# Computing the B path one step further ahead of its scan in a fused convolution-attention kernel

## The chip, the cores and the metric

The kernel runs on one core of a Trainium2 chip. The metric is the device time of one execution in microseconds, median over several executions. The kernel before took 1475.62 us (median of 3 executions, 1474.55 to 1480.86; a fourth, 1480.84, puts the median at 1478.23 in the result below).

Engines: PE is TensorE (matmuls), PEld its weight loads, DVE is VectorE, ACT is ScalarE, POOL is GpSimd, SP is SyncE, which issues 971 of the 993 transfers in the trace before.

## The reference, cut to what matters

```python
x = x + conv(_gn(x), ...)                  # GroupNorm, 32 groups, then layer 0
t = tokens(x)
t = t + attn(_ln_t(t), ...)                # linear attention, no softmax
t = t + ffn(_ln_t(t), ...)                 # FFN with quantised products

def conv(x, ...):                          # per position: LayerNorm, then one projection
    proj = layernorm(x) @ W_in + b_in      # -> value u, gate g, delta d, and A, B, C (96*16 each)
    def step(h, (A, B, C, d, u, g)):       # over 4096 positions
        h = d * (A * h) + d * (B * u)
        y = g * sum_S(C * h)
    return ys @ W_out + b_out
```

The input is 4 batches x 4096 positions x 96 channels. Each batch is worked in 8 chunks of 512 positions, and each chunk in 12 tiles, because the 96 x 16 = 1536 states of a position fill twelve sets of 128 partitions. That makes 32 chunks and 384 tiles; one step of the main loop scans one tile.

## The kernel before

For each tile PE projects A, B and C (three matmuls each) into PSUM, one bank for each letter. ACT copies B from its bank to a `bu` tile in SBUF, POOL multiplies that by `du` (d times u, replicated by DMA), DVE multiplies A by d, scans, and multiplies C by the result.

```python
    def b_copy(self):                                      # ACT
        self.bu = work.tile([P, TC], F32, tag="bu", name=f"bu_{self.nm}", bufs=4)
        nc.scalar.activation(self.bu, self.b_ps, AF.Identity, bias=self.bias(0))
    def b_mul(self):                                       # POOL
        nc.gpsimd.tensor_tensor(
            self.bu, self.bu, rep["du4", self.b, self.i, self.cg], ALU.mult
        )
    def scan(self):                                        # DVE
        ...
        nc.vector.tensor_tensor_scan(
            self.h, self.a_ps, self.bu,
            0.0 if self.i == 0 else state[self.sh, self.cg], ALU.mult, ALU.add,
        )
...
        while s < K or any(q >= s for q in steps):
            ...
            if 0 <= s + 1 < K:
                tiles[s + 1].a_proj()
            if 0 <= s < K:
                tiles[s].c_proj()
            if 0 < s <= K:
                last.keep()
            if 0 <= s + 1 < K:
                tiles[s + 1].b_mul()
            if 0 <= s < K:
                last = tiles[s]
                last.scan()
            if 0 <= s + 1 < K:
                tiles[s + 1].a_mul()
            if 0 <= s < K:
                last.c_mul()
            call(s)                  # the other work due at this step: norms, gate, FFN, ...
            if 0 <= s + 2 < K:
                tiles[s + 2].b_proj()
                tiles[s + 2].b_copy()
            s += 1
```

Two pieces of the "other work" matter below. The first is LayerNorm. `rstd` is computed on POOL, `nmr` (minus mean times rstd) on DVE, and ACT normalises with both. There are three LayerNorms per chunk: c (on `z`, ahead of the projections), a (ahead of attention) and f (ahead of the FFN). The second is GroupNorm's square root, which POOL does as a power of -0.5 once per batch.

```python
    def rsqrt(dst, var, eps):
        nc.gpsimd.tensor_scalar(dst, var, eps, None, ALU.add)
        nc.gpsimd.tensor_tensor(dst, dst, mhalf[:, : dst.shape[1]], ALU.pow)
...
        def apply(self, dst, src):                         # LayerNorm
            nmr = small.tile([P, J], F32, tag="nmr", name=f"nmr_{self.nm}")
            nc.vector.scalar_tensor_tensor(
                nmr, self.mv[:, :, 0], -1.0, self.r, ALU.mult, ALU.mult
            )
            for j in range(J):
                nc.scalar.activation(
                    dst[:, j, 0:C], src[:, j, :], AF.Identity,
                    bias=nmr[:, j : j + 1], scale=self.r[:, j : j + 1],
                )
...
        def root():                                        # GroupNorm of the next batch
            gnr[b] = small.tile([P, G], F32, tag="gnr", name=f"gnr_{b}", bufs=2)
            rsqrt(gnr[b], v["w"], 1e-5)
```

Of the kernel before, what the change touches and what calls it, by code (L numbers as in the profile page):

```python
# [8 lines left out]
F32 = mybir.dt.float32  # L9
# [7 lines left out]
P = 128  # L17
# [5 lines left out]
TC = P * J  # L23
# [21 lines left out]
def conv_attn_hybrid_kernel(  # L45
# [212 lines left out]
    work = ctx.enter_context(tc.tile_pool(name="work", bufs=2))  # L258
# [269 lines left out]
    class Tile:  # L528
# [18 lines left out]
            self.b_ps = self.proj("B", w_b)  # L547

        def b_copy(self):
            self.bu = work.tile([P, TC], F32, tag="bu", name=f"bu_{self.nm}", bufs=4)  # L550
            nc.scalar.activation(self.bu, self.b_ps, AF.Identity, bias=self.bias(0))  # L551

        def b_mul(self):
# [38 lines left out]
    tiles = {}  # L592
# [193 lines left out]
    K = N * NT  # L786
# [16 lines left out]
    def call(step):  # L803

        todo = steps.get(step, [])
        n = 0
        while n < len(todo):
            fn, args = todo[n]
            fn(*args)
            n += 1  # L810

    with tc.manual_schedule():
        s = FRONT
        while s < K or any(q >= s for q in steps):
            for k in (s, s + 1, s + 2):
                if 0 <= k < K and k not in tiles:
                    tiles[k] = Tile(k)
            if 0 <= s + 1 < K:
                tiles[s + 1].a_proj()
            if 0 <= s < K:  # L820
                tiles[s].c_proj()
            if 0 < s <= K:
                last.keep()
            if 0 <= s + 1 < K:
                tiles[s + 1].b_mul()
            if 0 <= s < K:
                last = tiles[s]
                last.scan()
            if 0 <= s + 1 < K:
                tiles[s + 1].a_mul()  # L830
            if 0 <= s < K:
                last.c_mul()
            call(s)
            if 0 <= s + 2 < K:
                tiles[s + 2].b_proj()
                tiles[s + 2].b_copy()
            s += 1


# [30 lines left out]
```

## Time and profile before

| | before |
|---|---|
| median, us | 1475.62 |
| profiled span, us | 1471.2 |
| busy share PE / DVE / POOL / ACT | 92% / 82% / 54% / 47% |
| first scan starts at, us | 119.4 |
| scan's waits for POOL's bu, us | 70.2 |
| PE weight loads' waits for ACT's bu copy, us | 32.2 |

The busy share says which engine has least idle time, but not whether a given wait costs anything: a wait counts only if what follows it is late at the end. So the useful unit here is the length of a chunk, taken as the distance between the starts of every twelfth scan. I number these stretches from 0 by scan start, so that stretch 20 starts at 909.60 us in the kernel before. (The prediction's windows are cut at other points; its timeline near 901 us lies at the end of stretch 19.) Three pairs (5+6, 13+14, 21+22) hold GroupNorm's root and what follows it. The other stretches from 10 on, eighteen of them, I call late, those from 0 to 4 and 7 to 9 early. The prediction shows the lines themselves.

### The profile page before, as it was taken

The page shows a single profiled execution, that of the slowest core. Times are in us where ns is not written, and L with a number is a line of the kernel's source. Part 1 is how long each engine was busy: PE and PEld are TensorE (multiplying, and loading weights), DVE is VectorE, ACT ScalarE, POOL GpSimd, SP SyncE. Part 2 cuts the span into 40 slices and gives each one's busy share as a digit, 9 for nine tenths or more (in the row PEclk, how much of TensorE's full clock was granted, in tenths as well). Part 3 has the DMA queues.
Part 4 walks back from the last instruction along what each step waited for, and adds up shares of the span by engine and source line. Part 5 has one row for each costly group of instructions (what it writes and reads, how often), then busy time and mean ns, then how long its engine had stood idle before and what let it go on. Part 6 is the DMA issues. An engine that isn't in the chain of part 4 may idle for free.

```text
span 1471.2 us, 20878 instructions
## 1 busy us (share of the span) xinstructions
PE 1350.2 (92%) x6513; PEld 910.4 (62%) x6513; DVE 1205.1 (82%) x2295; ACT 697.5 (47%) x1573; POOL 795.0 (54%) x772
## 2 busy tenths in 40 slices
PE   5747999998999999999999999999999999999875
PEld 4615666665666666666666666666666666666552
DVE  1017999997999999988998999988999999999743
ACT  2023344342333565544555555554555555555555
POOL 4234555555554556656655555666555655555424
PEclk9559999999999999999999999999999999999955
DMA  7102222221222222211222222221222222222001
GB/s 185 27 17 61 57 61 64 63 58 38 53 54 56 64 64 59 69 46 42 58 58 51 62 69 63 60 58 39 52 54 58 56 49 54 53 58 49 11 7 43
DMA packets 82209, 80.98 MB, mean 55 GB/s; under 512 B 49899, under 2 KB 50383, under 8 KB 82098
## 3 DMA queue, kind: packets, MB, share of 16 engines
q1 hardware_dynamic: 80080, 77.22, 22.1%
q10 hardware_dynamic: 2018, 2.43, 0.7%
q8 instruction: 51, 0.84, 0.2%
q14 instruction: 60, 0.49, 0.1%
HBM read 8.72 MB, written 6.29 MB: 10 GB/s over the span
## 4 chain that ended last, share of the span: by engine, by line
PE 57%; DVE 12%; ACT 11%; issue 6%; SPq 5%; POOL 4%; DMA 3%; ACTq 0%; POOLq 0%; DVEq 0%
PE Bps L155 13%; PE Cps L155 12%; PE Aps L155 11%; PE y_ps L601 5%; SPq L487 4%; DVE h L570 4%; PE dug_ps L155 3%; DVE ch L588 3%; POOL bu L554 3%; ACT z L305 3%; PE a_ps L705 2%; ACT xn L305 2%; ACT bu L551 2%; PE o_ps L624 2%; DMA d<-d 1%
## 5 line engine op out<-in xcount | busy, mean ns | idle before, releaser
L554 POOL TENSOR_TENSOR bu<-bu,du 128x512 f32<-128x512 f32 x384 | 493.6, 1286 | 536.9 <-ACT bu L551 382.2
L570 DVE TENSOR_TENSOR_SCAN h<-Aps,state,bu 128x512 f32<-128x512 f32 x336 | 428.2, 1274 | 58.3 <-POOL bu L554 57.5
L551 ACT ACTIVATE bu<-Bps,b_bac 128x512 f32<-128x512 f32 x384 | 261.8, 682 | 430.8 <-PE Bps L155 407.0
L563 DVE SCALAR_TENSOR_TENSOR Aps<-Aps,b_bac,d 128x512 f32<-128x512 f32 x384 | 283.9, 739 | 42.8 <-PE Aps L155 42.1
L155 PE MATMUL Bps<-xs,w 128*128 128x512 f32 x768 | 272.1, 435 | 15.0 <-ACT bu L551 15.0
L588 DVE SCALAR_TENSOR_TENSOR ch<-Cps,b_bac,h 128x512 f32<-128x512 f32 x384 | 285.6, 744 | 0.1
L155 PE MATMUL Aps<-xs,w 128*128 128x512 f32 x768 | 243.7, 398 | 13.1 <-DVE h L570 13.0
L155 PE MATMUL Cps<-xs,w 128*128 128x512 f32 x768 | 248.3, 404 | 4.0 <-DVE ch L588 4.0
L155 PEld LDWEIGHTS Bps<-xs,w 128*128 128x128 f32 x768 | 128.0, 191 | 79.0 <-ACT bu L551 32.2
L155 PEld LDWEIGHTS Aps<-xs,w 128*128 128x128 f32 x768 | 144.7, 189 | 49.6 <-DVE h L570 15.7
L155 PEld LDWEIGHTS Cps<-xs,w 128*128 128x128 f32 x768 | 139.7, 189 | 53.2 <-DVE ch L588 23.7
L155 PE MATMUL Cps<-xl,w 128*128 128x512 f32 x384 | 152.5, 397 | 0.0
L155 PE MATMUL Bps<-xl,w 128*128 128x512 f32 x384 | 152.4, 397 | 0.0
L155 PE MATMUL Aps<-xl,w 128*128 128x512 f32 x384 | 152.4, 397 | 0.0
L601 PE MATMUL y_ps<-ch,fold 128*32 128x512 f32 x768 | 136.4, 605 | 0.0
L305 ACT ACTIVATE xa<-x,nmr_a,rstd_a 128x96 f32<-128x96 f32 x128 | 49.4, 457 | 112.5 <-DVE nmr_a L301 112.5
L305 ACT ACTIVATE z<-z,nmr_c,rstd_c 128x96 f32<-128x96 f32 x128 | 49.4, 457 | 80.4 <-DVE nmr_c L301 80.4
L155 PEld LDWEIGHTS Aps<-xl,w 128*128 128x128 f32 x384 | 72.4, 188 | 18.0
L155 PEld LDWEIGHTS Cps<-xl,w 128*128 128x128 f32 x384 | 72.5, 189 | 17.7
L155 PEld LDWEIGHTS Bps<-xl,w 128*128 128x128 f32 x384 | 72.7, 189 | 17.2
L743 ACT ACTIVATE hq<-hr 128x512 fp8e5<-128x512 f16 x96 | 60.6, 631 | 17.9 <-PE y_ps L749 9.4
L155 PE MATMUL dug_ps<-xs,w_dug 128*96 128x512 f32 x192 | 64.0, 415 | 5.3 <-DMA xs<-lo 4.9
(158 smaller groups left out, 1704.3 us busy)
## 6 DMA issues: line engine op xcount, KB each, us to landing
d<-d SPq DMA_DIRECT2D x384, 64.0 KB, 2.0
du<-du SPq DMA_DIRECT2D x384, 64.0 KB, 2.0
xl<-lo SPq DMA_DIRECT2D x64, 128.0 KB, 2.3
x<-in_x_dram SPq DMA_DIRECT2D x32, 192.0 KB, 2.8
out_dram<-o SPq DMA_DIRECT2D x32, 192.0 KB, 2.1
w<-w SPq DMA_DIRECT2D x18, 128.0 KB, 2.3
xs<-lo SPq DMA_DIRECT2D x32, 64.0 KB, 2.0
raw<-in_L_conv_W_in_dram ACTq DMA_DIRECT2D x3, 576.0 KB, 5.2
```

The source lines that it names most:

```text
L155: nc.tensor.matmul(ps, lhsT=wt[:, n], rhs=mv, start=(n == 0), stop=(n == 2))
L305: nc.scalar.activation(dst[:, j, 0:C], src[:, j, :], AF.Identity, bias=nmr[:, j : j + 1], scale=self.r[:, j : j + 1],)
L487: nc.sync.dma_start(t[q * 32 : (q + 1) * 32, :], src[cg * 32 : (cg + 1) * 32, :])
L551: nc.scalar.activation(self.bu, self.b_ps, AF.Identity, bias=self.bias(0))
L554: nc.gpsimd.tensor_tensor(self.bu, self.bu, rep["du4", self.b, self.i, self.cg], ALU.mult)
L563: nc.vector.scalar_tensor_tensor(self.a_ps, self.a_ps, self.bias(1), rep["d4", self.b, self.i, self.cg], ALU.add, ALU.mult,)
L570: nc.vector.tensor_tensor_scan(self.h, self.a_ps, self.bu, 0.0 if self.i == 0 else state[self.sh, self.cg], ALU.mult, ALU.add,)
L588: nc.vector.scalar_tensor_tensor(self.ch, self.c_ps, self.bias(2), self.h, ALU.add, ALU.mult)
L601: nc.tensor.matmul(y_ps[g][cg * 32 : (cg + 1) * 32, :], lhsT=fold, rhs=tiles.pop(g * NT + NCG * sh + cg).ch, start=(sh == 0), stop=(sh == ...
L624: nc.tensor.matmul(ps[:, j, :], lhsT=yg[:, j * P : (j + 1) * P], rhs=w_o, start=True, stop=True)
L705: nc.tensor.matmul(ps[:, j, :], lhsT=xa[:, j, :], rhs=rmat[b], start=True, stop=True)
L743: nc.scalar.activation(v["hq"][:, m, :], v["hr", m], AF.Copy, saturate=False)
```

## The change

The intent is to give the scan a whole step of slack towards POOL. Projection, copy and multiplication of B each move one tile ahead, in the same places of the loop, and the ring of `bu` tiles grows by one to hold the tile that now lives one step longer.

```diff
         def b_copy(self):
-            self.bu = work.tile([P, TC], F32, tag="bu", name=f"bu_{self.nm}", bufs=4)
+            self.bu = work.tile([P, TC], F32, tag="bu", name=f"bu_{self.nm}", bufs=5)
 ...
-            for k in (s, s + 1, s + 2):
+            for k in (s, s + 1, s + 2, s + 3):
 ...
-            if 0 <= s + 1 < K:
-                tiles[s + 1].b_mul()
+            if 0 <= s + 2 < K:
+                tiles[s + 2].b_mul()
 ...
-            if 0 <= s + 2 < K:
-                tiles[s + 2].b_proj()
-                tiles[s + 2].b_copy()
+            if 0 <= s + 3 < K:
+                tiles[s + 3].b_proj()
+                tiles[s + 3].b_copy()
```

## The prediction

> **What bounds the kernel now.** I read the first part of the page, then two windows of one chunk each (a chunk is 512 positions, twelve tiles, one tile a step; 32 chunks), then the costliest groups, the waits, and last the timeline of one chunk. First the engines over the span, and the windows of chunk 20 (late, with the FFN of the previous batch beside it) and chunk 3 (early, without); columns are length, then busy us of PE, PEld, DVE, ACT, POOL:
>
> ```profile
> PE 1350.2 (92%) x6513; PEld 910.4 (62%) x6513; DVE 1205.1 (82%) x2295; ACT 697.5 (47%) x1573; POOL 795.0 (54%) x772
> 891.80:932.00 40.20, 39.74 (x201) 26.20 (x200) 36.61 (x69) 22.71 (x53) 24.27 (x25) 1.00 0.26 63
> 212.95:250.74 37.79, 37.17 (x174) 24.11 (x174) 34.78 (x60) 15.23 (x38) 21.31 (x20) 1.00 0.26 62
> ```
>
> In a chunk PE is marked busy 99% (39.74 of 40.20) and DVE 91%. DVE therefore has 3.6 us of idle time per chunk and PE seems to have 0.5. POOL, which does the multiplication that the change moves, is busy 60%. The waits, each with its total in us, its count and its longest:
>
> ```profile
> POOL bu L554 <- ACT bu L551: 382.2, 184, 5.5
> DVE h L570 <- POOL bu L554: 70.2, 64, 8.2
> PEld Bps L155 <- ACT bu L551: 32.2, 65, 3.5
> PEld Cps L155 <- DVE ch L588: 23.7, 66, 0.9
> POOL bu L554 <- DMA du<-du: 14.8, 7, 7.9
> ```
>
> POOL waiting for ACT costs nothing by itself, since POOL has time. The scan (h) waits 70.2 us for POOL, and that is the wait the change aims at. PE's own waits are smaller. The timeline of chunk 20 shows how they hang together:
>
> ```profile
> 900.84 1.28 DVE L570 TENSOR_TENSOR_SCAN h<-Aps,state,bu 128x512 f32<-128x512 f32 x1 [0.98 <-POOL bu L554]
> 901.69 7.55 SPq L487 DMA_DIRECT2D du<-du  x12
> 903.35 0.15 DVE L301 SCALAR_TENSOR_TENSOR nmr_c<-mv_c,rstd_c 128x4 f32<-128x4 f32 x1
> 903.53 1.54 ACT L305 ACTIVATE z<-z,nmr_c,rstd_c 128x96 f32<-128x96 f32 x4 [2.27 <-DVE nmr_c L301]
> 904.99 0.67 ACT L551 ACTIVATE bu<-Bps,b_bac 128x512 f32<-128x512 f32 x1
> ...
> 905.70 0.30 PEld L155 LDWEIGHTS Bps<-xs,w 128*128 128x128 f32 x2 [0.50 <-ACT bu L551]
> 905.73 1.29 POOL L554 TENSOR_TENSOR bu<-bu,du 128x512 f32<-128x512 f32 x1 [2.25 <-ACT bu L551]
> 907.06 1.28 DVE L570 TENSOR_TENSOR_SCAN h<-Aps,state,bu 128x512 f32<-128x512 f32 x1 [0.95 <-POOL bu L554]
> 908.26 0.30 PEld L155 LDWEIGHTS Bps<-xs,w 128*128 128x128 f32 x2 [0.26 <-ACT bu L551]
> 908.28 1.30 POOL L554 TENSOR_TENSOR bu<-bu,du 128x512 f32<-128x512 f32 x1 [0.41 <-ACT bu L551]
> ```
>
> A late scan (900.84) makes nmr_c late; ACT, in order, waits for it and normalises z (1.54) before it copies the next B (0.67); PE waits for that copy, because B has one PSUM bank; POOL multiplies (1.29) only then, and the scan at 907.06 is late again. So in the last four steps of a chunk the B chain (ACT, POOL, scan) sets DVE's pace and takes a little from PE; elsewhere PE is limiting, and DVE waits for it. Early chunks have one such scan, and there PE pays through C's single bank:
>
> ```profile
> 226.75 1.28 DVE L570 TENSOR_TENSOR_SCAN h<-Aps,state,bu 128x512 f32<-128x512 f32 x1 [0.88 <-POOL bu L554]
> 229.39 0.30 PEld L155 LDWEIGHTS Cps<-xs,w 128*128 128x128 f32 x2 [0.65 <-DVE ch L588]
> ```
>
> [...] PEld is only 62% busy, and a matmul marked busy 0.39 us is followed by the next after 0.23 us (900.07 to 900.30), so the mark hides stalls such as the 0.50 above. I therefore count PE's stalls from the starts of its matmuls. [...] the 0.95 us before the scan does repeat, but the binding buffer for PE is B's PSUM bank, which the change leaves at one. [...] here the du copies take 2.0 from issue to landing (median, 1.9 to 3.7), so the transfer matters if the multiplication comes earlier.
>
> **The change, part by part.** It adds and removes no instruction: 384 projections, copies and multiplications stay at about 0.70, 0.69 and 1.29 us. It costs one more 2 KB-per-partition tile.
> (1) At step s, POOL multiplies tile s+2 instead of s+1, ACT copies s+3 instead of s+2, PE projects s+3. In each engine's queue these stand where they stood; only the tile number moves by one. So the scan gets one step (at least 2.5 us: scan 1.20, A 0.64, C 0.66 from start to start) of slack. The largest routine wait is 0.98 us, so nearly all of the 70.2 us should go; one of 8.2 us lies in the start and may stay.
> (2) What of it reaches the end? DVE has idle time anyway, so what counts is PE's stalls that follow from late scans. Taking for each pair of consecutive matmul groups the 10th percentile of their distance as unstalled, a late chunk loses in its last steps 0.47 us (at 905.70) and 0.24 us (at 908.26), that is 0.71. Without the 0.98 before the scan at 900.84, nmr_c comes about 0.8 earlier (its A and C are there at 901.2 and 901.9, so not the whole 0.98), the copy ends near 904.9 instead of 905.66, and PE, free near 905.2, does not wait. Then the second stall goes too, ACT's cycle (2.55 from copy to copy) being close to PE's (2.43). I find the pair in 17 late chunks, others at a batch's edges have none or part: 17 x 0.71 + 0.6 = 12.7 us.
> (3) Early chunks: C's wait for c_mul costs 0.49 us (the 0.65 of PEld, less what overlaps), in chunks 1 to 8: 8 x 0.49 = 3.9 us. B's stall there (about 0.6) comes from nmr_c with no late scan before it, and stays.
> (4) Left as they are: PE's wait for a copy after xn (0.45 of PEld at 899.49 in late chunks, nmr_f being on time), for xa (0.6 a chunk), half-clock stretches, the drain after the last scan.
> (5) The start: the first tile's du still lands at 117 us, so perhaps 1 us is gained there, which I take against the costs below.
> Sum: 12.7 + 3.9 = 16.6, some 17 us.
>
> **What may be paid.** The first multiplication of a chunk needs du, and now one step earlier. In chunk 20 the first four of the twelve du copies, issued from 901.69 at 0.63 each, land at 904.95 by the trace's landings; the multiplication started at 908.28, and takes in future the place of the one at 905.73: 0.8 us to spare. Other late chunks have from -0.7 to +0.8; early ones -0.3 to -1.3. So POOL will wait there for DMA in many chunks, 0.3 to 1.3 us, and the second and third du tiles follow 3 us apart. The scan has a whole step in hand, so this should be hidden; what POOL does behind it (centring for GroupNorm, four chunks a batch) comes later and may hold ACT some tenths: 1 to 3 us in all.
>
> **Rivals.** (A) DVE, or the chain through it, is the real bound: then all of the waits count, 70.2 - 8.2 = 62 us, and the time is near 1414. For it: the chain that ended last passes POOL's bu for 2.8% and the scan for 3.9% of the span. Against: the same chain is 57% PE, and after such stretches DVE waits 42 us for A from PE. A half-way case, with stalls after xn and in the early B also gone (about 0.45 x 20 + 0.6 x 8 = 14 us more), gives 1445.
> (B) The du transfer takes the place of the removed wait, POOL stays late over three tiles, and scans wait as before: gain 0 to 5, near 1472. For it: the landings above. Against: a step of slack remains, and POOL has 40% idle.
> (C) PE is so full that only the half of my stalls is recovered, others (xa, A) growing in their place: about 1467.
>
> **Range and chances.** 1475.6 - 17 = 1458.6; with 1 us of net start gain less costs I stay at 1459. B and C set the upper end at 1471, the half-way A the lower at 1443. Faster by over 2% needs less than 1446.1, that is more than 29 us, almost all of PE's stalls on B and C: 0.13. Slower by 2% would need a new stall of almost 1 us in every chunk, for which nothing speaks: 0.02. Within 2%: 0.85.
>
> **What would show it.** In the changed profile: the scan's wait for POOL below 15 us (step 1). PEld's wait for ACT's bu falling from 32 to about 17 us and for C's c_mul from 23.7 to below 12 (steps 2, 3). POOL's wait for du rising from 14.8 to 20 to 40 us (costs). DVE's waits for A from PE rising from 42 by tens of us, since the idle time moves from before the scan to before A: this would say that PE is the bound, and against A. The late chunk between equal points goes from 40.2 to 39.5 us. I am wrong if the scan still waits for POOL, if the time falls by over 29 us though PE's stalls as I counted them were only 17, or if ACT's copy gets later and PE's wait for it grows.

## The result, and the profile after

| | before | after |
|---|---|---|
| median, us (range, runs) | 1478.23 (1474.55 to 1480.86, 4) | 1462.09 (1459.15 to 1466.46, 4) |
| ratio (95%) | 1 | 0.9895 (0.9857 to 0.9933) |

A ratio is, to within 0.0004, the mean time of one kernel's fast runs over the mean of the other's fast runs of the same rounds, so it is not quite the ratio of the medians. The outputs are correct. The time fell by about 1%, inside the range and 3 us from the predicted value. The total came out close, but the terms of the sum did not.

**A caution first: two ways to start.** Executions of either kernel fall into two groups. Most have a mean granted clock below 0.96; of these, eight were profiled, and seven start their first scan at 118 to 121 us, one (e5_ring_only, described below) at 124.4. Some have 0.966 or more; the four profiled ones start it at 127 to 128, and in most series such runs take 5 to 7 us longer in all (kernel before in its last series: 1481.1 late, 1474.6 early; in e7c_all only 2.5). What sets their mean clocks apart lies before the first scan: each of the eight early records has a stretch of 68 or 75 us at half clock there, and none of the four late ones has. I call the two groups early and late starters; the early one is itself spread over some 6 us (1472.8 to 1479.3 for the kernel before). The profiled execution of the kernel after is one of the late starters (first scan at 127.2), that of the kernel before is not (119.4). I therefore compare from the first scan to the end, 1351.8 us before (1471.2 - 119.4) and 1337.5 after (1464.7 - 127.2): **14.3 us less**. Where times are compared below, I also give the mean of the early-start runs.

Engines and waits of the kernel after (each wait with total us, count, longest):

```profile
PE 1354.2 (92%) x6513; PEld 916.4 (63%) x6513; DVE 1217.9 (83%) x2295; ACT 697.1 (48%) x1573; POOL 794.7 (54%) x772
```

```profile
POOL bu L554 <- DMA du<-du: 87.8, 40, 7.9
DVE Aps L563 <- PE Aps L155: 71.7, 104, 5.2
PEld Bps L155 <- ACT bu L551: 32.5, 66, 4.2
PEld Cps L155 <- DVE ch L588: 16.2, 43, 0.9
DVE h L570 <- POOL bu L554: 13.7, 6, 3.4
```

The wait that the change aims at fell from 70.2 to 13.7 us, and DVE's idle time moved to A, which it gets from PE (42.1 to 71.7). But PE's wait for the B copy is what it was, 32.2 and now 32.5. So PE's largest repeated stall was not touched, although the prediction took most of its gain from there.

Where the 14.3 us came from, by stretches:

| stretches | before, us | after, us | difference |
|---|---|---|---|
| 0 to 4 and 7 to 9 (early) | 299.4 | 295.2 | -4.3 |
| 10 to 12, 15 to 20, 23 to 31 (late) | 710.9 (no. 12 40.15, no. 28 39.19) | 710.3 (no. 12 40.11, no. 28 39.15) | -0.6 |
| 5+6 | 82.27 | 79.88 | -2.4 |
| 13+14 | 87.08 | 83.22 | -3.9 |
| 21+22 | 86.00 | 83.23 | -2.8 |
| after the last scan | 86.16 | 85.81 | -0.35 |

Nine of the fourteen come from three places that the prediction had left out, and almost nothing from the eighteen late chunks. Two windows each show it; columns are length, then busy us of PE, PEld, DVE, ACT, POOL, then the granted clock, DMA share and GB/s. Before, stretches 13+14 and 20:

```profile
621.50:708.58 87.08, 81.65 (x396) 54.84 (x394) 74.72 (x143) 44.88 (x105) 51.56 (x47) 0.96 0.21 51
909.60:949.78 40.18, 39.67 (x202) 26.20 (x200) 36.59 (x69) 22.71 (x54) 24.27 (x24) 1.00 0.26 63
```

After, the same:

```profile
622.60:705.82 83.22, 79.13 (x395) 52.47 (x394) 75.34 (x144) 44.78 (x104) 51.08 (x48) 1.00 0.22 53
906.59:946.68 40.09, 39.61 (x201) 26.29 (x200) 37.25 (x70) 22.70 (x54) 24.39 (x25) 1.00 0.27 64
```

The late chunk has the same length and the same PE time, with DVE 0.66 us *busier* (36.59 to 37.25), though it does the same instructions. The other pair is 3.86 us shorter, with the clock at 1.00 in place of 0.96.

**Late chunks.** The end of a late chunk after the change (the place of the prediction's timeline at 901 us):

```profile
899.99 1.28 POOL L554 TENSOR_TENSOR bu<-bu,du 128x512 f32<-128x512 f32 x1
900.35 0.94 DVE L301 SCALAR_TENSOR_TENSOR nmr_c<-mv_c,rstd_c 128x4 f32<-128x4 f32 x1
901.32 1.55 ACT L305 ACTIVATE z<-z,nmr_c,rstd_c 128x96 f32<-128x96 f32 x4 [2.28 <-DVE nmr_c L301]
902.78 0.66 ACT L551 ACTIVATE bu<-Bps,b_bac 128x512 f32<-128x512 f32 x1
903.49 0.30 PEld L155 LDWEIGHTS Bps<-xs,w 128*128 128x128 f32 x2 [0.50 <-ACT bu L551]
```

The scan is in time, yet ACT still waits 2.28 us for nmr_c (2.27 before), and PE still waits 0.50 for the copy. What is new is nmr_c itself: an operation on 4 elements per partition takes 0.94 us, where it took 0.15. It ends at 901.29, when POOL's multiplication ends (901.27). All 32 of them, min/median/max in ns, first in the kernel before:

```profile
L301 DVE SCALAR_TENSOR_TENSOR nmr_c<-mv_c,rstd_c x32: 150/158/842, 96.3 to 1304.6; 128x4 f32<-128x4 f32 x32
```

and in the kernel after:

```profile
L301 DVE SCALAR_TENSOR_TENSOR nmr_c<-mv_c,rstd_c x32: 150/930/952, 104.1 to 1298.4; 128x4 f32<-128x4 f32 x32
```

In every late chunk of both kernels that has an nmr_c, it ends 16 to 26 ns after a POOL multiplication ends. Before the change, the late scan pushed DVE's work back so far that it reached nmr_c only at that moment, so the record showed a short instruction. After it, DVE comes some 0.8 us earlier (0.930 less 0.158) and stands there.

nmr_c reads two tensors of SBUF (mean and rstd); A's multiplication, the scan and C's multiplication read one each besides PSUM. In the kernel after, the medians of these three differ by at most 11 ns beside POOL: A's is 732 ns over the 62 that lie more than 95% inside a POOL multiplication and 739 over the 165 that meet none; the scan's is 1275 (9) and 1272 (82), C's 751 (38) and 740 (130). nmr_c's are 940 (19) and 153 (7). nmr_f, of the same form, takes 1.11 and 1.13 us the two times that it starts early in a multiplication, and ends 16 and 24 ns after it. So the wait may belong to the form with two SBUF inputs, but so far that is only an argument, and why such a form would wait the traces don't show.

**GroupNorm's root.** At one step of each of the first three batches POOL computes the root for the next batch. Before:

```profile
662.81 5.46 POOL L279 TENSOR_TENSOR gnr<-gnr,mhalf 128x32 f32<-128x32 f32 x1
...
669.53 1.28 DVE L570 TENSOR_TENSOR_SCAN h<-Aps,state,bu 128x512 f32<-128x512 f32 x1 [4.57 <-POOL bu L554]
670.87 1.18 PE L155 MATMUL Aps<-xs,w 128*128 128x512 f32 x2 [2.60 <-DVE h L570]
```

After:

```profile
663.74 5.46 POOL L279 TENSOR_TENSOR gnr<-gnr,mhalf 128x32 f32<-128x32 f32 x1
...
670.48 1.28 DVE L570 TENSOR_TENSOR_SCAN h<-Aps,state,bu 128x512 f32<-128x512 f32 x1 [3.02 <-POOL bu L554]
671.82 0.73 PE L155 MATMUL Aps<-xs,w 128*128 128x512 f32 x2 [0.53 <-DVE h L570]
```

A power on 32 columns takes 5.46 us, and the next multiplication stands behind it. The scan waited 4.57 us, and PE, whose A bank is freed by the scan, 2.60. With the lead these are 3.02 and 0.53. Before, the pair of matmuls after the gap takes 1.18 us instead of 0.73, since the clock is at half there (0.50 granted from 671.0 to 674.4 us). Such stretches last 3.413 us in the traces; the kernel before has five in mid-run (near 333, 353.5, 650.5, 671.0 and 998.6 us), the kernel after one (near 337.5). In the window of 13+14 the clock of 0.96 comes from two such stretches.

The traces show what goes before them. In the three with the old order (before, and e5_ring_only and e1c_before_nmrc, described below) PE stands 2.57 to 2.64 us at each of the three roots, and half clock follows all nine times. In the three with the new order (the change twice, e6_lead_ring4) that gap is 1.8 us at the first root and under 1.5 at the others, and no half clock follows. The remaining stretches follow another gap, of 2.32 or 2.33 us and a little earlier, in which PE waits for a GroupNorm sum from DVE (`gsq`). That gap is in all six traces; half clock follows it seven times in nine with the old order and three in nine with the new.

An estimate of what one stretch costs: 0.9 us, from pair 21+22, which is 86.00 us with one stretch (before) and 86.87 with two (e5); or 1.5, from e2c_after_nmrc and e7c_all, which have none in 13+14 and one in 21+22 (82.49 and 83.96, 80.32 and 81.85), where the change with none in either has 83.22 and 83.23. Four stretches fewer are then 3.5 to 6 of the 9.0 us. The rest I put down to the shorter waits themselves; no run separates the two.

### The profile page after: what moved, and what is told of

Read it like the earlier page. It is cut to its first block, busy times and chain, and to the rows that moved or that the text cites. A ratio compares the mean times of both kernels' runs of the same rounds, so it can differ in the third digit from the quotient of the medians.

```text
span 1464.7 us, 20864 instructions
## 1 busy us (share of the span) xinstructions
PE 1354.2 (92%) x6513; PEld 916.4 (63%) x6513; DVE 1217.9 (83%) x2295; ACT 697.1 (48%) x1573; POOL 794.7 (54%) x772
## 5 line engine op out<-in xcount | busy, mean ns | idle before, releaser
L554 POOL TENSOR_TENSOR bu<-bu,du 128x512 f32<-128x512 f32 x384 | 493.4, 1287 | 520.4 <-ACT state L580 312.2
L563 DVE SCALAR_TENSOR_TENSOR Aps<-Aps,b_bac,d 128x512 f32<-128x512 f32 x384 | 285.2, 743 | 72.4 <-PE Aps L155 71.7
L155 PE MATMUL Cps<-xs,w 128*128 128x512 f32 x768 | 245.2, 400 | 3.3 <-DVE ch L588 3.3
L155 PEld LDWEIGHTS Bps<-xs,w 128*128 128x128 f32 x768 | 127.4, 191 | 79.1 <-ACT bu L551 32.5
L155 PEld LDWEIGHTS Cps<-xs,w 128*128 128x128 f32 x768 | 140.7, 188 | 47.7 <-DVE ch L588 16.2
```

Of the source, the lines that this page charges most:

```text
L155: nc.tensor.matmul(ps, lhsT=wt[:, n], rhs=mv, start=(n == 0), stop=(n == 2))
L554: nc.gpsimd.tensor_tensor(self.bu, self.bu, rep["du4", self.b, self.i, self.cg], ALU.mult)
L563: nc.vector.scalar_tensor_tensor(self.a_ps, self.a_ps, self.bias(1), rep["d4", self.b, self.i, self.cg], ALU.add, ALU.mult,)
```

## The experiments

**Theory 1**: the late chunks gained nothing because nmr_c, as an operation with two SBUF inputs, has to wait for POOL's multiplication; where the scan's wait was, there is now this one. **Rival 1**: PE's two stalls belong to ACT's order and B's single bank as such, and nothing done to nmr_c helps; or any earlier nmr_c would have helped the kernel before too, so that it has nothing to do with the change. **Theory 2**: about 9 us come from the root on POOL. **Rival 2**: they come from the fifth ring tile, or from which executions were profiled. Runs of one series were made on the same chip with the same runs of the kernel before.

### The change again

a0_after_again is the changed kernel, unaltered, in the first series.

> The changed kernel once more, so that the others of this call have it on the same chip. Both theories: ratio to before 0.987 to 0.992 (1.0 to 1.3% less). In its trace: scan waiting for POOL about 14 us, PE loads of B waiting for ACT's copy about 32 us (unchanged), nmr_c with a median of about 0.93 us where before had 0.16. The profiled run of the change began its first scan 7.8 us later than the one of before; if that was chance, the first scan is here near 119 us and the span near 1457 us.

Measured: 1466.64 us (1461.82 to 1467.31), ratio 0.9927 (0.9905 to 0.9948), against 1475.55. Four of the six runs were late starters. The profiled run was again one of them (first scan at 126.8), and with them the ratio just misses the 0.987 to 0.992 that I expected. The other two have a mean of 1461.9 us and those of the kernel before 1475.7 (10 of 11): 13.8 us, near the trace's 14.3. So a few late starts move a median by 5 us. Over both series the five early-start runs of the changed kernel have a mean of **1461.4**, which I compare with from here on.

### Theory 1: nmr without the second SBUF input

The first form changes all three LayerNorms of the changed kernel. The rstd becomes a per-partition scalar of four one-column operations (label e2_after_nmr):

```diff
-            nc.vector.scalar_tensor_tensor(
-                nmr, self.mv[:, :, 0], -1.0, self.r, ALU.mult, ALU.mult
-            )
+            for j in range(J):
+                nc.vector.tensor_scalar(
+                    nmr[:, j : j + 1], self.mv[:, j, 0:1], self.r[:, j : j + 1], -1.0,
+                    ALU.mult, ALU.mult,
+                )
```

> The changed kernel, with the LayerNorm's small product nmr (mean times rstd, two SBUF tensors of 128x4) made by four tensor_scalar operations that read one SBUF tensor each and take rstd as a per-partition scalar. Theory (nmr_c is held up by POOL's multiplication[...]): the four end within 0.4 us of c_mul, the normalisation of z begins about 0.8 us earlier against the scan, the two PE stalls at the end of a late chunk (0.5 and 0.25 us of load wait) go, a late chunk falls from 40.1 to 39.4 us, and the time is 10 to 13 us below the changed kernel (ratio to before about 0.981). Rival (nmr_c waits for POOL's result or for ACT[...]): the operations start 0.8 us later instead of lasting longer, late chunks stay at 40.1 us, and the time is the changed kernel's, within 0.3%.

Measured: 1456.99 us, ratio 0.9882; early-start mean 1456.3, so 5.1 us below the change. Late chunk no. 12 fell from 40.11 to 39.77. The direction is that of theory 1, the size half of it: the end of a chunk gained 0.70, but 0.37 were lost elsewhere. The four operations take 0.55 us where nmr_f, which met at most the last tenths of a POOL multiplication in these chunks, had taken 0.13 to 0.26; so the f LayerNorm, on PE's path in another step, became later. A sharper edit was needed: only LayerNorm c, `ln.apply(v["t"], v["t"], True)`, the other two as they were. This was put on the changed kernel (e2c_after_nmrc) and on the kernel before (e1c_before_nmrc):

```diff
-        def apply(self, dst, src):
+        def apply(self, dst, src, one_input=False):
...
+            if one_input:
+                ...                          # the four tensor_scalar as above
+            else:
+                ...                          # the one scalar_tensor_tensor
...
-        at(s + 7, lambda: ln.apply(v["t"], v["t"]))
+        at(s + 7, lambda: ln.apply(v["t"], v["t"], True))
```

> The changed kernel with the product nmr made by four one-input operations for the z LayerNorm alone, the two others as they were. In the run with all three, PE's stalls at the end of a late chunk went (0.70 us a chunk), but 0.37 us came back before the transposes of xn, because nmr_f took longer. Theory [...]: without that a late chunk falls from 40.13 to about 39.4 us and the time, at an early start, from 1461.9 to about 1449 (12 to 14 us less, ratio to before about 0.982). Rival (the gain of that run came from the xn and xa norms starting after the first of four pieces): no more gained than there, ratio 0.988 or more.

> The same four operations in the kernel before. Theory: there c_mul, held back by the scan's wait for POOL, ends just when POOL's multiplication does, [...] the change of nmr gains nothing or loses up to 5 us (ratio 0.999 to 1.004), late chunks stay at 40.1 to 40.4. So neither the change nor this alone helps late chunks; both together do. Rival (the nmr form is a gain of its own, apart from the change): 10 us or more gained here too, ratio under 0.994.

Measured: on the change 1449.17 us, ratio 0.982 (0.9801 to 0.9839), all four runs early starters with a mean of 1448.9: **12.5 us** below the change. On the kernel before: 1474.9, ratio 1.0004 (0.9984 to 1.0024), nothing. The end of a late chunk in e2c_after_nmrc:

```profile
885.22 1.28 POOL L561 TENSOR_TENSOR bu<-bu,du 128x512 f32<-128x512 f32 x1
885.58 0.57 DVE L303 TENSOR_SCALAR nmr_c<-mv_c,rstd_c 128x1 f32<-128x1 f32 x4
885.82 1.54 ACT L312 ACTIVATE z<-z,nmr_c,rstd_c 128x96 f32<-128x96 f32 x4 [1.54 <-DVE nmr_c L303]
...
888.11 0.42 PEld L155 LDWEIGHTS Bps<-xs,w 128*128 128x128 f32 x2
```

POOL multiplies from 885.22 to 886.50; nmr_c starts beside it at 885.58 with 0.2 us a piece, and z starts after the first piece. ACT's wait is 1.54 instead of 2.28, and PE's load at 888.11 has no wait behind it where 0.50 stood. The late chunk is 39.38 us (no. 12) instead of 40.11 and 38.42 (no. 28) instead of 39.15, 0.73 in both. Over all eighteen late stretches the traces give 11.8 us (710.3 to 698.5), against 12.5 in the time. PE's loads wait 20.8 us for the B copy in all, where the change alone had left 32.5. So these are the stalls of 0.71 that the prediction had counted, and nmr_c's wait for POOL's multiplication was what had kept them. And e1c shows that nmr_c's form alone is worth nothing while the scan is late: no. 12 is 40.20 there. The late scan and this wait each cover the other; only removing both pays. Rival 1 falls in both forms.

### A second step of lead

If POOL were not multiplying at all when nmr_c comes, the original two-input form should be short as well. One more step of lead changes what POOL does there (e8_lead2; the ring stays at five, and in its trace a copy never starts less than 3.3 us after the end of the scan that frees its tile):

```diff
-            if 0 <= s + 2 < K:
-                tiles[s + 2].b_mul()
+            if 0 <= s + 3 < K:
+                tiles[s + 3].b_mul()
 ...
-            if 0 <= s + 3 < K:
-                tiles[s + 3].b_proj()
-                tiles[s + 3].b_copy()
+            if 0 <= s + 4 < K:
+                tiles[s + 4].b_proj()
+                tiles[s + 4].b_copy()
```

> The changed kernel with B one further step ahead (multiplied three steps before its scan, copied four), still with a ring of five. Theory (a first step of lead takes every routine wait away; what is left for a second is the rest of the waits at the three batch edges, about 3 us each in the changed kernel): the scan's waits for POOL after the start go, 2 to 6 us are gained on the changed kernel (ratio 0.986 to 0.9895), late chunks stay at 40.1 us. Rival (lead as such is short, also in late chunks): a late chunk falls below 39.8 us and 8 us or more are gained.

Measured: 1460.8 us, ratio 0.9886, mean 1460.9 (all six early). This series was run on another chip, where the kernel before has 1474.6; so the gain is 13.7 us, against 14.3 for the change (1475.7 to 1461.4), and none of the 2 to 6 us that I expected on top. (The ratio looks better because six of its eleven runs of the kernel before were late starters.) But the equality hides two opposite moves, and my expectation for the late chunks was wrong too. The end of a late chunk:

```profile
897.38 0.15 DVE L301 SCALAR_TENSOR_TENSOR nmr_c<-mv_c,rstd_c 128x4 f32<-128x4 f32 x1
...
900.47 1.30 POOL L554 TENSOR_TENSOR bu<-bu,du 128x512 f32<-128x512 f32 x1 [3.41 <-DMA du<-du]
```

POOL stands from 897.06 to 900.47 and waits for the chunk's first du, the two-input nmr_c takes 0.15 us in that time, and the late chunk without GroupNorm work is 38.44 (no. 28), as with e2c's edit (38.42): a third view of the same cause, without touching nmr_c. It also answers a rival to e2c, that the gain came only from z starting after the first of four pieces: here nmr_c is one piece. Chunks with GroupNorm's centring behind that wait got longer (40.68 to 41.94 for no. 10 to 12), since POOL's centring is late then and ACT, in order, waits for it before its square:

```profile
ACT sq L390 <- POOL xc L385: 42.1, 12, 4.6
```

POOL's waits for du are 178.9 us in total here, against 87.8 with one step. So a lead has a price in du, which is hidden at one step and shows at two.

### Theory 2: the root cut in four

On the kernel before (e3_before_split) and on the change (e4_after_split), the power is cut into four of 8 columns, one in each of four steps, so that a multiplication can go in between:

```diff
-            rsqrt(gnr[b], v["w"], 1e-5)
+            nc.gpsimd.tensor_scalar(gnr[b], v["w"], 1e-5, None, ALU.add)
+
+        def power(n):
+            c = slice(n * 8, (n + 1) * 8)
+            nc.gpsimd.tensor_tensor(gnr[b][:, c], gnr[b][:, c], mhalf[:, c], ALU.pow)
...
         at(e + 3, root)
+        for n in range(4):
+            at(e + 3 + n, power, n)
```

> The kernel before, with the one power of GroupNorm at a batch's edge (128x32 on POOL, 5.46 us) cut into four of 8 columns in four successive steps. Theory (at three batch edges POOL is shut for 5.46 us, the scan waits 4.6 us and PE 2.6 us, often with half clock after it; this is where most of the change's gain comes from): the scan's waits of over 2 us at the edges go, and 8 to 11 us are gained against before (ratio 0.993 to 0.9945). Rival (the gain comes from the routine waits in each chunk, and the edges only look large): under 3 us gained, ratio over 0.998.

> The changed kernel with the same cut of the power. Theory: the change has already taken two thirds of the edges' cost, so only 1 to 4 us are gained against the changed kernel (ratio to before 0.986 to 0.9885), and against the cut kernel of before the change is then worth 4 to 8 us instead of 15. Rival (routine waits carry the gain): the change is worth its full 15 us on top of the cut.

Measured: before plus cut 1465.21 us, ratio 0.9931 (0.9911 to 0.9952), early-start mean 1464.7: 11.0 below the kernel before. Change plus cut 1453.28, ratio 0.986, mean 1453.8: 7.6 below the change, more than I expected. The place in e3_before_split:

```profile
659.63 1.67 POOL L435 TENSOR_TENSOR gnr<-gnr,mhalf 128x8 f32<-128x8 f32 x1
661.27 1.29 POOL L560 TENSOR_TENSOR bu<-bu,du 128x512 f32<-128x512 f32 x1
662.60 1.28 DVE L576 TENSOR_TENSOR_SCAN h<-Aps,state,bu 128x512 f32<-128x512 f32 x1 [0.81 <-POOL bu L560]
```

The scan waits 0.81 us where it waited 4.57, and stretch 13 is 44.15 us instead of 48.03 (42.31 with the change). By the traces the cut takes 10.2 us from the three pairs (82.27, 87.08 and 86.00 become 78.86, 83.17 and 83.12) and leaves early and late stretches as they were. So the cut alone recovers about what the change recovers there, 9.0, by another way, and the mechanism of theory 2 holds.

My accounting for the two together was too simple, however. I expected them to overlap almost wholly at the roots, so that the change on top of the cut would be worth 4 to 8 us. It is worth 10.9 by the means (1464.7 to 1453.8) and 10.1 by the traces: 4.4 in the early stretches, 3.4 in the pair 5+6 (78.86 to 75.44), 1.1 in the other two pairs, 0.7 late and 0.6 in the drain. The excess sits at the first root: the trace of e3 has a half-clock stretch there (0.91 over 320 to 340 us), and that of e4 has none. By the estimate above that is worth 0.9 to 1.5 of the 3.4, and two early chunks at some 0.5 each (4.4 over eight) are another 1.1; the rest, about 1 us, I can't explain from one trace of each.

### The ring and the order, each alone

e5_ring_only is the kernel before with `bufs=5`; e6_lead_ring4 is the changed kernel with `bufs=4`.

> The kernel before with a ring of five bu tiles and the old order. Theory: in the trace of before, ACT's copy never comes within 6.6 us of the end of the scan that frees its tile, so the ring was not waited for and the time is that of before (ratio 0.998 to 1.002). Rival (the fifth tile gives part of the gain): ratio under 0.997.

> The changed order with the old ring of four. In the changed kernel's trace the copy starts at least 3.3 us after the end of the scan four tiles back, so a ring of four would never be waited for either. Theory (the order alone carries the gain, the fifth tile is not needed): as the changed kernel, ratio 0.988 to 0.993. Rival (the lead needs the tile): the gain falls to less than half, ratio over 0.996.

Measured: ring alone 1476.95 us, ratio 1.0006 (0.9988 to 1.0024): nothing. Order alone 1461.58, ratio 0.9907 (0.9889 to 0.9925), all six early with a mean of 1461.7, so all of the gain. The scan's wait in e6 falls as in the full change:

```profile
DVE h L570 <- POOL bu L554: 13.9, 6, 3.4
```

The trace tells why the fifth tile is not needed: in the changed order, the copy into tile k never starts less than 3.05 us after the end of scan k-4, which frees a ring of four; against scan k-3 it would start up to 1.7 us too early, so three would not do. The ring half of rival 2 falls. So does the other half, that the 9 us hang on which executions were profiled: three traces with the old order (before, ring alone, one-input nmr_c on before) have the pairs at 82.24 to 82.53, 87.08 to 87.29 and 86.00 to 86.87 us, and three with the new order (the change twice, and with a ring of four) at 79.88 to 79.91, 83.22 to 83.30 and 83.20 to 83.29.

### All together

e7c_all is the change with e2c's edit and the cut root.

> The three together: the changed kernel, the z product nmr by one-input operations, GroupNorm's power cut into four. Theory: the last two act in different places (end of late chunks, batch edges) and add up: 12.5 us and 8 us less than the changed kernel, so about 1441 us at an early start, ratio to before 0.976 to 0.979. Rival (they remove the same stalls): ratio over 0.980.

Measured: 1443.04 us (1442.03 to 1445.24, 4 runs), ratio 0.9761 (0.9736 to 0.9787), early-start mean 1442.7 against 1474.6. It is the fastest version: 2.4% below the kernel before by the ratio, 2.2% by the early-start means, as six of the eleven runs of the kernel before were late starters here. PE's wait for the B copy is 20.5 us and the scan's for POOL 4.4.

| kernel | ratio to before | early-start mean, us | late chunk no. 12 / 28, us |
|---|---|---|---|
| before | 1 | 1475.7; 1474.6 in the last series | 40.15 / 39.19 |
| ring of five alone | 1.0006 | 1476.7 | |
| one-input nmr_c alone | 1.0004 | 1474.9 | 40.20 / - |
| cut root alone | 0.9931 | 1464.7 | 40.16 / 39.21 |
| the change (again) | 0.9927 | 1461.4 (both series) | 40.11 / 39.15 |
| the change, ring of four | 0.9907 | 1461.7 | |
| second step of lead (last series) | 0.9886 | 1460.9 | 40.75 / 38.44 |
| change + one-input nmr, all three | 0.9882 | 1456.3 | 39.77 |
| change + cut root | 0.986 | 1453.8 | 40.09 / 39.17 |
| change + one-input nmr_c | 0.982 | 1448.9 | 39.38 / 38.42 |
| change + both (last series) | 0.9761 | 1442.7 | 39.38 / 38.43 |

## Why the prediction was right or wrong

The total was right (1459 predicted, 1462.09 measured, 14.3 us from the traces against 16.6 in the sum), and "within 2%" was right. A term of 12.7 was missing almost wholly and a term of 9.0 stood in for it by chance.

- **Step 1, the scan gets its slack: right.** 70.2 us of waits went to 13.7, below the 15 named; the one long wait left at each root is 3.0 to 3.4.
- **Step 2, late chunks 12.7 us: wrong, measured 0.6.** The failing sentence is "Without the 0.98 before the scan at 900.84, nmr_c comes about 0.8 earlier". DVE did come that much earlier, but nmr_c then waited for POOL's multiplication and ended when it had ended before. The prediction took nmr_c's 0.15 us from its record and did not ask why it ended, in every late chunk, some 20 ns after a POOL multiplication. The size of the stall (0.71 a chunk) was right: e2c recovered 0.73, once nmr_c no longer waited for POOL's multiplication.
- **The roots: missed, measured 9.0.** The prediction said that the chunks at a batch's edges "have none or part" of the 0.71, gave them 0.6 in all, and took half-clock stretches as left as they are; they went from five to one. The trace held the clue: the scan waits 4.57 us at the root, far above the routine 0.98, and half clock follows.
- **Step 3, early chunks 3.9: right**, measured 4.3. In stretches 1 to 4, 7 and 8, six of its eight chunks, it is 0.53 each against 0.49, and the loads' wait for c_mul in the early stretches fell from 9.4 to 5.3 us. In all it fell from 23.7 to 16.2, though not below the 12 named.
- **Step 4, what stays: right** for the drain (within 0.35 us) and for PE's wait for copies after xn, wrong for half clock (see the roots). **Step 5, the start:** no gain is to be seen under two start modes that differ by 7 us.
- **Costs: too small in the wait, too large in time.** POOL's wait for du went to 87.8, not 20 to 40. One reading behind it was wrong: 904.95 is the landing of the third of the first tile's four du copies; the fourth, issued at 903.59, lands at 905.56, so only 0.2 us was to spare and not 0.8. POOL's waits for ACT before its multiplications fell at the same time, from 506.5 us (382.2 and 124.3) to 403.6 (312.2 and 91.4). So the wait for du mostly took the place of a wait for ACT, and no net loss shows in the late stretches (-0.6): the 1 to 3 us that I took for it were not paid.
- **Rivals.** A (the DVE chain is the bound, 1414) is false: DVE's idle time moved to A, as the prediction said it would if PE is the bound. B (du takes the wait's place) is false: the scan's wait did not stay. A's half-way case (1445) is false too: in the early stretches PE's loads wait 6.5 us for the B copy before and 6.2 after. C (half of the stalls recovered, 1467) comes within 5 us of the total but hasn't the cause: late chunks recovered none.
- **What would show it:** the late chunk at 39.5 and PE's B wait at 17 both failed plainly (40.1 and 32.5). The prediction was right to name them, since the total alone would have hidden the error.

What stays open: why nmr_c's two-input form waits for POOL's multiplication, how much of the gain at the roots is clock and how much is the waits themselves, about 1 us at the first root when it is cut, and why the clock drops after some gaps of 2.3 us and not after others.

## What to carry to other kernels

Before counting on an instruction to come earlier, find what its *end* coincides with: a short instruction that always ends just after another engine's may be waiting for it already, and will show its wait once its own lateness is taken away. A removed wait is worth something only if the next one behind it is removed too, and the two together (here -27 us for order and nmr_c, where nmr_c alone gave nothing) are worth more than their sum. When a total agrees with a prediction, check each term on the stretches it was meant for.

## What else the runs show

- nmr_c in its two-input form, on 128x4, takes 0.94 us (median of 19) where it lies inside POOL's 1.28 us multiplication and 0.15 where it meets none, and ends 17 to 23 ns after that multiplication (kernel after); four one-column pieces of 0.2 us run beside it.
- Half clock in mid-run comes in stretches of 3.413 us. In twelve traces between the first scan and the drain, it followed all 11 gaps of 2.57 to 2.64 us, 20 of 34 gaps of 2.31 to 2.33, and none of 28 between 1.55 and 1.88.
- A power on POOL takes 1.03 us for 128x4, 1.64 for 128x8 and 5.46 for 128x32.
- One program starts in two ways: in the late one the first scan starts some 7 us later and small matmuls near 40 us take longer (0.57 us for a pair in place of 0.36), while the granted clock in the records shows no drop there (1.00 over 30 to 50 us in the trace after).
